# A reciprocal root changes places with a product in GpSimd's list

## The chip, the cores and the metric

The kernel runs on one core of one Trainium2 chip. The time is the device time of one execution in microseconds (us), as the median of several runs; lower is better. The engines are called PE (TensorE), DVE (VectorE), ACT (ScalarE), POOL (GpSimd) and SP (SyncE, which only starts transfers here). Each works through a list of its own in order and waits for the others through semaphores.

## The reference

Two layers over x of 16 sequences, 256 tokens, 128 features, in float32. Each layer is attention, then a feed-forward part; each part takes a layer norm scaled and shifted by a modulation, and adds its gated result to x. The first layer has softmax attention and 16 experts. The second, where the change lies, is

```
# holographic attention of layer 1, 16 heads of 64
k = exp(1j * (x @ Wk) * 10);  v = x @ Wv;  rotors = exp(1j * t * freqs)
out_pos   = real(cumsum(v * rotors) * conj(rotors)) / sqrt(t)
out_assoc = real(cumsum(v * conj(roll(k, 1))) * k) / sqrt(t)
x = x + ga * ((out_pos * g_pos + out_assoc * g_assoc) @ Wo)
# token mixing of layer 1
h = layernorm(x) * (1 + cb) + sb
x_prev = h shifted by one token
r = sigmoid((mu_r*h + (1-mu_r)*x_prev) @ W_r)
k = (mu_k*h + (1-mu_k)*x_prev) @ W_k
x = x + gb * (r * (square(relu(k)) @ W_v))
```

"The mixing" is this last part, and "its figures" are the mean and the reciprocal standard deviation of its layer norm.

## The kernel before

The 16 sequences are worked as 8 chunks of two (`NCH = 8`). Three stages follow each other: layer 0's attention, layer 0's experts, and layer 1 with both of its parts. The third runs from about 688 us to the end and is one loop over 58 steps `n`, each a chunk `c` and a group `j` of 128 of the 1024 head features. Chunks 0 to 5 have 7 groups here (one and a half of their groups were done ahead, in the experts' stage, and come back through `fetched`), chunks 6 and 7 have 8. The seventh group of chunks 0 to 5 is a half step (`is_half`): only its associative part is left.

In this stage all four engines' lists are in the order in which the code emits them (`manual_schedule(engines=IN_ORDER)`, line 1175). So the place of a call in the loop body is its place in the engine's list. For a step `n` the loop emits

- DVE: `summed` (L1238) twice, the running sums of the associative and of the positional binding; `phases(n + 2)` (L1213), the phase `off` of a later step; the product `m_pos` (L1450).
- POOL: the product `m` of step n - 1 (L1456), called `sum_assoc` in the profile; then `binders(n + 1)` (L1235), `bound_pos` and `bound_assoc` of the next step (a half step has only the latter). All are 128 x 1024.
- ACT: `cosines(n + 2)` (L1219 to L1221) makes the phasor from `off`, and `projected(n + 3)` (L1198, L1202) copies keys and values out of PSUM.
- PE: `out_project` for both products (L1252, into one accumulator per chunk) and the projections of step n + 3 (L1197, L1201). The next chunk's first `out_project` needs the accumulator, which `gated_out` on ACT (L1277, `oT`) reads out at j = 0.

Between these the mixing of earlier chunks is spread out: `place` maps a number of steps since a chunk's attention ended to that chunk, and each number has its piece of the mixing. Number 2 is `mix_means` (ACT, L204 and L205: sums of x and minus the mean, `less_f`). Number 3 is `mix_figures` (ACT, L213 to L221: sums of squares, then the variance plus epsilon, `off_f`). Number 4 is `mix_spread` (POOL, L228 the power of -1/2, called the root here, `rstd_f`; L229 its product with `less_f`). Number 5 is `mix_norm` (ACT, L236 through `normed`: `hn_f`). Then follow transposes (6), projections (7, 8, 9), gating (10, 11) and the output (12, 13).

`mix_spread` of number 4 is called near the end of the loop body, so its two small instructions come in POOL's list between the binders of one step and the product of the next. It is called for chunks 0 to 6 in this way. Chunk 7, the first to be mixed into x, has a call of its own at n = 5, and layer 0's stage calls the same function for the first layer norm of layer 1.

Of the kernel before, what the change touches and what calls it, by code (L numbers as in the profile page):

```python
# [55 lines left out]
def tile_adaln_two_layers(ctx: ExitStack, tc: tile.TileContext, a: dict, out: bass.AP):  # L56
# [167 lines left out]
    def mix_spread(c, pool):  # L224

        less, off = mix[c]
        rstd = pool.tile([P, 4], F32, tag="rstd_f1", name=f"rstd_f1_{c}")
        nc.gpsimd.tensor_tensor(rstd, off, neg_half4, ALU.pow)  # L228
        nc.gpsimd.tensor_tensor(less, less, rstd, ALU.mult)  # L229
        mix[c] = rstd, less  # L230
# [936 lines left out]
    with ExitStack() as scope:  # L1167
        hp = scope.enter_context(tc.tile_pool(name="holo", bufs=2))
# [54 lines left out]
        def is_half(n):  # L1223

            return steps[n][0] < AHEAD and steps[n][1] == NJ - 2
# [4 lines left out]
        def binders(n):  # L1230
            w = work[n]
            v2 = w["v"].unsqueeze(1).to_broadcast(both)
            for nm, bind in (("pos", rot(n)), ("assoc", phasor[n % 3][:, :, :, 0:T]))[is_half(n) :]:
                w[nm] = hp.tile(both, F32, tag=f"bound_{nm}", name=f"bound_{nm}_{n}")
                nc.gpsimd.tensor_tensor(w[nm], v2, bind, ALU.mult)  # L1235
# [101 lines left out]
        def mix_gated(c, k):  # L1337
            pv, r = mix[c], mix[c, "r"]
            nc.vector.tensor_tensor(r[:, k, :], pv[:, k, :], r[:, k, :], ALU.mult)
# [78 lines left out]
        for n in range(last + 2):  # L1418
# [3 lines left out]
            place = {n - begin[m + 1]: m for m in (c - 2, c - 1) if 0 <= m < NCH - 1 and n <= last}  # L1422
# [30 lines left out]
            if 1 <= n <= last + 1:  # L1453
                m = work.pop(n - 1)["m"]
                part = slice(1 if is_half(n - 1) else 0, 2)
                nc.gpsimd.tensor_tensor(m[:, part], m[:, part], phasor[(n - 1) % 3][:, part, :, 1:], ALU.mult)  # L1456
            if n + 1 <= last:
                binders(n + 1)
            if 1 <= n <= last + 1:
# [73 lines left out]
            for k in range(2):  # L1533
                if 10 + k in place:
                    mix_gated(place[10 + k], k)
            if 4 in place:
                mix_spread(place[4], hp)
            if 11 in place:
                py = with_tokens_first(place[11], mix.pop((place[11], "r")), "py2")
            for k in range(2):  # L1540
# [118 lines left out]
```

## Time and profile before

| | |
|---|---|
| median of three runs | 1080.41 us (1078.15, 1080.41, 1080.94) |
| the profiled execution | 1078.81 us |
| its span, first to last instruction | 1076.70 us |
| mean granted clock of PE | 0.996 |
| busy over the span | PE 1020.6 us (95%), DVE 912.8 (85%), POOL 796.8 (74%), ACT 704.4 (65%) |
| full products on POOL, spacing of their starts | about 2.13 us |
| root L228 on POOL, 15 in all | 0.997 to 1.274 us, median 1.024 |
| L229 on POOL, 15 in all | 0.20 us |
| distance of the roots at 851.10 and 894.92 | 43.82 us |

The span is what the trace covers; the execution's time has 2.11 us more around it. POOL's recorded durations overlap a little with the next start, so its speed is read from the distance of starts. A wait is the idle time of an engine ahead of an instruction, put down to the instruction elsewhere that ended last before it.

### The profile page before, as it was taken

How to read it: one execution, taken by the hardware profiler on the slowest of the kernel's cores; microseconds unless marked ns; L12 is line 12 of the kernel's file. 1: busy time of each engine (PE TensorE's matmuls, PEld its weight loads, DVE VectorE, ACT ScalarE, POOL GpSimd, SP SyncE). 2: the span in 40 equal slices, each digit the busy share in tenths (PEclk: the TensorE clock that was granted, in tenths of full speed). 3: DMA queues.
4: the chain of work that ended last, by engine and by line, in shares of the span. 5: the costliest groups of instructions: out<-in, count | busy, mean ns of one | idle time of the engine just before them, and what ended most of it. 6: DMA issues, size and time to landing. Idle time of an engine off the chain costs nothing.

```text
span 1076.7 us, 16224 instructions
## 1 busy us (share of the span) xinstructions
PE 1020.6 (95%) x5333; PEld 517.4 (48%) x5333; DVE 912.8 (85%) x1413; ACT 704.4 (65%) x1515; POOL 796.8 (74%) x754
## 2 busy tenths in 40 slices
PE   7999999999999999999999999898999999999987
PEld 5566666676654444444444434333344444444334
DVE  6679878998756798988878788999999999999995
ACT  3776677667656676687767755365676767767662
POOL 2245334533557678888878788899999999999992
PEclk9999999999999999999999999999999999999999
DMA  3102100000052222322322232100000000000000
GB/s 117 43 11 69 50 8 3 2 4 2 4 178 98 80 99 79 118 101 96 109 89 89 89 101 95 59 10 10 20 3 27 15 15 30 1 11 5 5 10 19
DMA packets 35538, 53.15 MB, mean 49 GB/s; under 512 B 8416, under 2 KB 23296, under 8 KB 35456
## 3 DMA queue, kind: packets, MB, share of 16 engines
q1 hardware_dynamic: 34912, 51.87, 14.9%
q8 instruction: 42, 0.69, 0.3%
q14 instruction: 40, 0.33, 0.1%
q10 hardware_dynamic: 544, 0.26, 0.1%
HBM read 46.34 MB, written 5.51 MB: 48 GB/s over the span
## 4 chain that ended last, share of the span: by engine, by line
PE 53%; POOL 20%; DVE 11%; ACT 8%; issue 6%; DMA 1%; SPq 0%; DVEq 0%; POOLq 0%; ACTq 0%
PE pg L808 6%; PE acc L833 6%; PE pup L810 6%; PE s L440 5%; PE st L474 5%; PE po L494 5%; PE pout L1252 4%; POOL bound_assoc L1235 4%; POOL sum_assoc L1456 4%; POOL bound_pos L1235 4%; POOL u L825 3%; DVE mem L1238 2%; DVE sum_assoc L1238 2%; PE pq L567 2%; PE pk L1197 1%
## 5 line engine op out<-in xcount | busy, mean ns | idle before, releaser
L482 ACT ACTIVATE exp<-st 128x512 f32<-128x512 f32 x256 | 132.2, 603 | 85.9 <-PE st L474 85.9
L452 DVE TENSOR_REDUCE maxima<-s 128x2 f32<-128x512 f32 x256 | 158.8, 683 | 25.9 <-PE s L440 25.6
L825 POOL TENSOR_TENSOR u<-u,wide 128x512 f32<-128x512 f32 x128 | 164.6, 1286 | 16.5 <-DVE u L824 7.4
L833 PE MATMUL acc<-u,w_dn 128*128 128x512 f32 x256 | 133.9, 605 | 6.1 <-POOL u L825 5.9
L1238 DVE TENSOR_TENSOR_SCAN sum_assoc<-keep,bound_assoc 128x1024 f32<-128x1024 bf16 (+1 forms) x58 | 125.8, 2168 | 12.8 <-POOL bound_assoc L1235 12.8
L808 PE MATMUL pg<-hT,w_gu 128*128 128x512 f32 x256 | 131.9, 597 | 0.8 <-DVE logits L674 0.4
L810 PE MATMUL pup<-hT,w_gu 128*128 128x512 f32 x256 | 130.7, 592 | 0.0
L814 ACT ACTIVATE u<-pup,b_gu 128x512 f32<-128x512 f32 x128 | 87.0, 680 | 63.6 <-PE pup L810 57.6
L1235 POOL TENSOR_TENSOR bound_assoc<-v,phasor 128x1024 f32<-128x1024 f32 x57 | 124.9, 2192 | 0.2 <-ACT phasor L1221 0.2
L818 POOL TENSOR_SCALAR u<-u 128x512 f32<-128x512 f32 x128 | 80.3, 628 | 59.6 <-ACT u L814 53.4
L812 DVE TENSOR_SCALAR g<-pg,b_gu 128x512 f32<-128x512 f32 x128 | 95.3, 745 | 32.7 <-PE pg L808 32.4
L1456 POOL TENSOR_TENSOR sum_assoc<-sum_assoc,phasor 128x1024 f32<-128x1024 f32 (+1 forms) x58 | 121.5, 2094 | 0.4 <-DVE sum_assoc L1238 0.3
L1238 DVE TENSOR_TENSOR_SCAN mem<-keep,bound_pos 128x1024 f32<-128x1024 bf16 x52 | 118.1, 2271 | 0.0
L1235 POOL TENSOR_TENSOR bound_pos<-v,rotor 128x1024 f32<-128x1024 f32 x51 | 111.7, 2189 | 0.0
L1252 PE MATMUL pout<-sum_assoc,w_assoc 128*128 128x512 f32 x228 | 108.1, 596 | 3.6 <-POOL sum_assoc L1456 3.6
L1252 PE MATMUL pout<-m_pos,w_pos 128*128 128x512 f32 x204 | 97.2, 599 | 15.0 <-ACT oT L1277 12.0
L817 ACT ACTIVATE pg<-g 128x512 f32<-128x512 f32 x128 | 76.3, 596 | 42.3 <-DVE g L812 41.9
L824 DVE SCALAR_TENSOR_TENSOR u<-u,pg 128x512 f32<-128x512 f32 x128 | 86.7, 677 | 11.9 <-POOL u L818 9.9
L1219 ACT ACTIVATE phasor<-off 128x512 f32<-128x512 f32 x56 | 35.1, 627 | 78.3 <-DVE off L1213 78.3
L474 PE MATMUL st<-qx,kx 32*128 32x256 f32 x1024 | 81.7, 387 | 1.2 <-DMA qx<-turned 1.1
L833 PEld LDWEIGHTS acc<-u,w_dn 128*128 128x128 f32 x256 | 46.7, 191 | 74.3 <-issue 42.9
L440 PE MATMUL s<-kx,qx 32*128 32x256 f32 x1024 | 78.1, 407 | 4.2 <-DVE kx L577 1.8
(301 smaller groups left out, 1910.0 us busy)
## 6 DMA issues: line engine op xcount, KB each, us to landing
wide<-scores SPq DMA_DIRECT2D x64, 512.0 KB
qx<-turned SPq DMA_DIRECT2D x256, 1.0 KB
there<-total SPq DMA_DIRECT2D x12, 256.0 KB
fetched<-there SPq DMA_DIRECT2D x12, 256.0 KB
w_gu<-in_gate_up_dram SPq DMA_DIRECT2D x8, 256.0 KB
out_dram<-x SPq DMA_DIRECT2D x16, 128.0 KB
x<-in_x_dram SPq DMA_DIRECT2D x14, 128.0 KB
w_dn<-in_down_dram SPq DMA_DIRECT2D x4, 256.0 KB
```

The source lines that it names most:

```text
L440: nc.tensor.matmul(s[g][:, i, :], qs[c][r][rows_, k, ts(i, P)], ks[c][rows_, r // NS, k, :], start=True, stop=True,)
L452: nc.vector.tensor_reduce(mx[:, :, g], s[g], AX.X, ALU.max, negate=True)
L474: nc.tensor.matmul(st[g][:, i, :], ks[c][rows_, r // NS, k, ts(i, P)], qs[c][r][rows_, k, :], start=True, stop=True,)
L482: nc.scalar.activation(e[:, g, :, :], st[g], AF.Exp, scale=QSCALE)
L808: nc.tensor.matmul(pg, w_gu[:, e, 0 : 2 * D : 2], h2, start=True, stop=True)
L810: nc.tensor.matmul(pu, w_gu[:, e, 1 : 2 * D : 2], h2, start=True, stop=True)
L825: nc.gpsimd.tensor_tensor(u, u, wide[n // SOME][:, n % SOME, :], ALU.mult)
L833: nc.tensor.matmul(accs[c], w_dn[:, e, :], work.pop(n), start=False, stop=(e == NE - 1))
L1235: nc.gpsimd.tensor_tensor(w[nm], v2, bind, ALU.mult)
L1238: nc.vector.tensor_tensor_scan(dst[:, half].rearrange("p s k t -> p (s k t)"), keep.rearrange("p (s k) t -> p s k t", k=2)[:, half].rearra ...
L1252: nc.tensor.matmul(pos[c], w[:, j, :], m[:, k, :, :].rearrange("p k t -> p (k t)"), start=(j == 0 and i == 0 and k == 0), stop=(c < NCH - ...
L1456: nc.gpsimd.tensor_tensor(m[:, part], m[:, part], phasor[(n - 1) % 3][:, part, :, 1:], ALU.mult)
```

## The change

The call of `mix_spread` for number 4 is taken out of the end of the loop body. The same call is made in the next step, where the chunk's number is 5, between the product L1456 of that step and `binders(n + 1)`.

```diff
                 nc.gpsimd.tensor_tensor(m[:, part], m[:, part], phasor[(n - 1) % 3][:, part, :, 1:], ALU.mult)
+            if 5 in place:
+                mix_spread(place[5], hp)
             if n + 1 <= last:
                 binders(n + 1)
...
-            if 4 in place:
-                mix_spread(place[4], hp)
             if 11 in place:
```

POOL's list around the root of one chunk, before and after:

```
before: bound_pos, bound_assoc | rstd_f, less_f | sum_assoc | bound_assoc of the half step
after:  bound_pos, bound_assoc | sum_assoc | rstd_f, less_f | bound_assoc of the half step
```

This holds at seven places (chunks 0 to 6). The calls for chunk 7 and in the experts' stage stay. The lists of the other engines have the same instructions in the same order; the first `hn_f` of each of the seven chunks carries a wait for POOL of its own, which before was covered by an earlier wait of ACT.

## The prediction

> **What bounds the kernel now.** I read the busy time of the engines by stage first. Every instruction that the change moves in a working place lies in the last stage, from 688 us on, so only that stage can gain.
>
> ```profile
> 688.00:1052.00 364.00, 337.05 (x831) 145.85 (x829) 350.81 (x283) 242.68 (x524) 356.61 (x183) 1.00 0.05 14
> ```
>
> The columns are the stretch, its length, and the busy us of PE, PE's weight loads, DVE, ACT and POOL. POOL is busy 356.61 of 364 us, DVE 350.81, PE 337.05. POOL comes nearest to setting the pace, so next I asked whom it waits for there (us in total, times, longest).
>
> ```profile
> POOL rstd_f L228 <- ACT off_f L221: 3.8, 5, 0.9
> POOL bound_assoc L1235 <- ACT phasor L1221: 0.2, 1, 0.2
> ```
>
> Nearly all of POOL's waiting is at the moved instruction: the root waits five times for ACT's off_f. The timeline shows one such place, on POOL, then on ACT (start, duration, instruction; in brackets the idle time before it).
>
> ```profile
> 889.86 2.22 POOL L1235 TENSOR_TENSOR bound_pos<-v,rotor 128x1024 f32<-128x1024 f32 x1
> 891.99 2.22 POOL L1235 TENSOR_TENSOR bound_assoc<-v,phasor 128x1024 f32<-128x1024 f32 x1
> 894.92 1.01 POOL L228 TENSOR_TENSOR rstd_f<-off_f,neg_half 128x4 f32<-128x4 f32 x1 [0.71 <-ACT off_f L221]
> 896.00 0.20 POOL L229 TENSOR_TENSOR less_f<-less_f,rstd_f 128x4 f32<-128x4 f32 x1
> 896.36 2.17 POOL L1456 TENSOR_TENSOR sum_assoc<-sum_assoc,phasor 128x1024 f32<-128x1024 f32 x1 [0.16 <-issue]
> 898.50 2.18 POOL L1235 TENSOR_TENSOR bound_assoc<-v,phasor 128x1024 f32<-128x1024 f32 x1
> ```
>
> ```profile
> 890.95 0.72 ACT L1221 ACTIVATE phasor<-off,half_pi 128x512 f32<-128x512 f32 x1
> 894.64 0.20 ACT L221 ACTIVATE off_f<-off_f 128x4 f32<-128x4 f32 x1
> 903.34 1.66 ACT L236 ACTIVATE hn_f<-x,less_f,rstd_f 128x128 f32<-128x128 f32 x4
> ```
>
> POOL stands 0.71 us until off_f ends at 894.84. The product behind it (L1456) had nothing to wait for: DVE's sums for it ended about 891.2. The five waits, read off the same timeline, begin before the roots at 807.29 (0.74), 851.10 (0.72), 894.92 (0.71), 938.92 (0.72) and 983.23 (0.93): 3.82 us. The roots at 763.51 and 1035.67 wait for nothing. The root at 724.78 is not moved.
>
> Last I asked who else is nearly late. Per chunk DVE waits once, for POOL, and PE once, for ACT:
>
> ```profile
> 907.12 2.29 DVE L1238 TENSOR_TENSOR_SCAN sum_assoc<-keep,bound_assoc 128x1024 f32<-128x1024 bf16 x1 [1.55 <-POOL bound_assoc L1235]
> 916.08 1.98 PE L1252 MATMUL pout<-m_pos,w_pos 128*128 128x512 f32 x4 [1.86 <-ACT oT L1277]
> 960.39 1.98 PE L1252 MATMUL pout<-m_pos,w_pos 128*128 128x512 f32 x4 [1.42 <-ACT oT L1277]
> 980.13 2.18 POOL L1235 TENSOR_TENSOR bound_assoc<-v,phasor 128x1024 f32<-128x1024 f32 x1 [0.24 <-ACT phasor L1221]
> 983.23 1.01 POOL L228 TENSOR_TENSOR rstd_f<-off_f,neg_half 128x4 f32<-128x4 f32 x1 [0.93 <-ACT off_f L221]
> ```
>
> This closes a loop per chunk: POOL's binder releases DVE, DVE's off releases ACT's cosines, values and oT, oT releases PE, PE's next projections pace ACT, ACT's off_f releases POOL's root.
>
> **The change, part by part.** It adds and removes no work. Seven pairs (L228 and L229, about 1.24 us) trade places on POOL with the product of one step earlier; no DMA moves and SP's list is the same. The other engines keep their order.
>
> *The wait taken away.* After the change POOL goes from the binder (end 894.2) straight into the product, 2.13 us by the spacing of the starts. Only then does it ask for off_f, which is by then 1.4 us old (2.13 less 0.71). So the five waits go: 3.82 us at most.
>
> *Who reads the root later.* less_f would end 0.71 us earlier than the product ended before (898.53), near 897.8. Its reader, ACT's hn_f, starts at 903.34. This edit costs nothing: 5.5 us of cover, filled by ACT's cosines and evictions. Without the cover ACT would stop at L236, with the next cosines behind it and POOL's binder behind those.
>
> *What is late next.* The loop has a part that doesn't pass through POOL: PE's list of a chunk, then pv to ACT's v and oT and back to PE. In the chunk at 960.39 PE itself was what ACT waited for, and its gap was 1.42 us, so I take 1.42 as the shortest hand-over. The other chunks' gaps are 1.86, 1.85 and 1.86 (at 828.26, 872.07 and 916.08), so PE can come forward by only 0.44, 0.43 and 0.44 there, and not at all at 960.39. Its whole lead is thus 0.44, 0.87, 1.31 and 1.31 us.
>
> POOL meets this two instructions ahead of the root, at the binder that needs ACT's cosine L1221, which PE's list paces. At 891.99 the cosine had ended at 891.67, so POOL was 0.32 behind it; in the row at 980.13, where POOL did wait, start less cosine's end (979.98) is 0.15. The difference, 0.17 us, is the slack; it is the same in the chunks at 848.18 and 935.99. So POOL's lead there can't exceed PE's by more than 0.17. Now chunk by chunk, POOL's lead:
>
> - root at 807.29: +0.74; next binder caps it at 0.44 + 0.17 = 0.61.
> - root at 851.10: 0.61 + 0.72 = 1.33; capped at 0.87 + 0.17 = 1.04.
> - root at 894.92: 1.04 + 0.71 = 1.75; capped at 1.31 + 0.17 = 1.48.
> - root at 938.92: 1.48 + 0.72 = 2.20. Here the next binder (942.28) is near its cosine too: ACT has hT's modulation in front of it and ends at 941.68, 0.60 ahead, so a slack of 0.45: capped at 1.31 + 0.45 = 1.76. The binder at 980.13 has no slack: capped at 1.31.
> - root at 983.23: 1.31 + 0.93 = 2.24.
>
> From there POOL has no gap until 1051.9, and DVE, which waits for POOL at 990.96 (1.35) and again up to 1049.84 (0.59), follows. So 2.24 of the 3.82 us are kept, 1.58 go into waits for the cosine. The 0.16 us marked "issue" behind one root I leave alone, since the list may be interrupted elsewhere.
>
> *Bounds.* If PE can't come forward at all, POOL keeps only the last 0.93. If PE's hand-over holds nothing, all 3.82 go, and the 0.16 and 0.24 at most with them: 4.22. I take 2.24, which the 1.42 row is nearest to.
>
> *A rule that would speak against it.* The product now starts 2.2 us earlier beside DVE and meets m_pos (893.85) instead of the scan alone. The Trainium skill (SBUF — State Buffer, "Who interferes with whom") states that a DVE instruction with two SBUF inputs and a GpSimd instruction that reads SBUF block each other for a whole instruction. Here m_pos takes its sum from PSUM, so by the rule too there is no block, and the sum stays; by the rule for two SBUF inputs it would be the last rival below. The trace's own row: of 58 products the longest lasts 2.230 us against a median of 2.181, whatever DVE ran.
>
> **The rivals.**
>
> *All of the gain.* ACT and PE follow POOL fully, because the 1.42 at 960.39 belongs to a chunk with other work in it (hT's modulation, two more norms). For: PE is busy 337 of 364 us, less than DVE. Against: PE's list between the gaps shows no idle time. It gives 3.82 to 4.22, so 1076.4.
>
> *The wait only moves.* The binders' cosine wait takes back all but the last root's part: 0 to 0.93 us, 1079.9. For: 0.17 us of slack. Against: PE's gaps do exceed 1.42.
>
> *Slower.* The product in its new slot is blocked by DVE's m_pos, or blocks it, one m_pos each (1.21 us) at seven roots: 8.5 less 2.2 gives +6.2, so 1086.6. It decides as soon as a product that starts within m_pos is stretched by over 0.3 us. Against: the product at 868.52 starts inside the m_pos of 868.10 and lasts 2.20.
>
> **How the numbers follow.** The profiled execution took 1078.81 us, 2.11 around its span of 1076.70; the sum gives 1076.57 for it. It lay 1.60 below the median of the three runs, 1080.41, which gives 1078.17 for a median. All four executions average 1079.58, less 2.24 is 1077.3. I forecast 1077.8, between the two.
>
> 0.3% is 3.24 us, about what a measurement of this kernel tells from no change. Forecast (gain 0.93 to 3.2): 0.50. All of the gain: 0.31. Only moved: 0.14. Slower: 0.05. The runs differ by 2.8 us among themselves, so about three in ten of the forecast's case would show as over 0.3%: 0.15, and nine in ten of the full gain: 0.28, in all 0.43 faster. Slower gets its 0.05 and 0.01 of the third case. The rest, 0.51, is within 0.3%. Range: from 1080.41 less 4.22 and 0.8 of scatter, 1075.4, to 1080.41 less 0.93 and 0.7 of scatter, 1080.2.
>
> **What would show it.** Right: no wait of rstd_f for off_f in the last stage; new waits of bound_assoc for phasor L1221 of some 0.1 to 0.5 us, five or six; PE's gap before pout near 1.4 in each chunk; a distance of roots of 43.4 us instead of 43.8. Wrong: no such waits and a gap before pout near 1.1 (all of the gain), products over 2.5 us (the lock), hn_f waiting for less_f, or root and off_f still waiting.

## The result and the profile after

| | before | changed |
|---|---|---|
| median, 22 runs each | 1080.2 us (1077.61 to 1084.27) | 1077.01 us (1075.34 to 1080.66) |
| ratio to before, 95% interval | | 0.9972 [0.9961, 0.9983] |
| span of the profiled execution | 1076.7 us | 1073.6 us |
| POOL's part of the last stage | 361.63 us | 359.07 us |

The changed kernel is faster by 0.28%, some 3.0 us (1.8 to 4.2 by the interval). The last row runs from the start of the stage's first `bound_pos` (690.58 and 690.01) to the start of the last full product (1052.21 and 1049.08). It leaves out the stages in front, which the change doesn't touch; 0.57 us of the 3.1 us between the two spans lie there. So 2.56 us were gained where the change is. Of the runs of the kernel before that stand beside the experiments below, one took 3632 us; it is left out of their ratios.

POOL's waits in the last stage, changed kernel (us in total, times, longest):

```profile
POOL bound_assoc L1235 <- ACT phasor L1221: 1.7, 4, 0.8
```

The line for `rstd_f` and `off_f` (3.8 us, five times) is gone. In its place the binder waits for the cosine: 1.7 us instead of 0.2. POOL's idle time accounts for the gain: 3.81 us of waits for `off_f` and a hole of 0.16 us (marked "issue") go, and the waits for the cosine grow by 1.42, from 0.24 to 1.66. That makes 2.55 us of the 2.56. The timeline of the chunk shown before, POOL and then ACT:

```profile
890.32 2.18 POOL L1235 TENSOR_TENSOR bound_assoc<-v,phasor 128x1024 f32<-128x1024 f32 x1 [0.25 <-ACT phasor L1221]
892.46 2.18 POOL L1456 TENSOR_TENSOR sum_assoc<-sum_assoc,phasor 128x1024 f32<-128x1024 f32 x1
894.59 1.01 POOL L228 TENSOR_TENSOR rstd_f<-off_f,neg_half 128x4 f32<-128x4 f32 x1
895.68 0.20 POOL L229 TENSOR_TENSOR less_f<-less_f,rstd_f 128x4 f32<-128x4 f32 x1
```

```profile
889.45 0.72 ACT L1221 ACTIVATE phasor<-off,half_pi 128x512 f32<-128x512 f32 x1
893.14 0.21 ACT L221 ACTIVATE off_f<-off_f 128x4 f32<-128x4 f32 x1
901.42 1.65 ACT L236 ACTIVATE hn_f<-x,less_f,rstd_f 128x128 f32<-128x128 f32 x4
```

The root now starts 1.24 us after `off_f` has ended (893.35) and has no idle time ahead of it. `less_f` ends at 895.88, 5.5 us before `hn_f` reads it. POOL stands 0.25 us at the binder, 0.14 us behind the cosine's end (890.175). PE at one gap before, and at three after:

```profile
872.07 1.98 PE L1252 MATMUL pout<-m_pos,w_pos 128*128 128x512 f32 x4 [1.85 <-ACT oT L1277]
```

```profile
870.57 1.98 PE L1252 MATMUL pout<-m_pos,w_pos 128*128 128x512 f32 x4 [1.42 <-ACT oT L1277]
913.91 1.98 PE L1252 MATMUL pout<-m_pos,w_pos 128*128 128x512 f32 x4 [1.42 <-ACT oT L1277]
958.23 1.98 PE L1252 MATMUL pout<-m_pos,w_pos 128*128 128x512 f32 x4 [1.42 <-ACT oT L1277]
```

The gaps of 1.85 and 1.86 have shrunk to 1.42, the one that had been 1.42 is still 1.42, and the first two rows after are 43.34 us apart instead of 44.0.

### The profile page after: what moved, and what is told of

Its sections match the earlier page's. It is cut to its first block, busy times and chain, and to the rows that moved or that the text cites. A ratio compares the mean times of both kernels' runs of the same rounds, so it can differ in the third digit from the quotient of the medians.

```text
span 1073.6 us, 16224 instructions
## 1 busy us (share of the span) xinstructions
PE 1020.8 (95%) x5333; PEld 518.4 (48%) x5333; DVE 913.2 (85%) x1413; ACT 705.0 (66%) x1515; POOL 796.7 (74%) x754
## 4 chain that ended last, share of the span: by engine, by line
PE 64%; POOL 15%; DVE 10%; issue 5%; ACT 5%; DMA 1%; SPq 0%; DVEq 0%; POOLq 0%; ACTq 0%
PE pout L1252 9%; PE pg L808 7%; PE acc L833 7%; PE pup L810 7%; PE s L440 5%; PE st L474 5%; PE po L494 5%; POOL u L825 3%; POOL bound_assoc L1235 3%; POOL bound_pos L1235 3%; POOL sum_assoc L1456 2%; PE pk L1197 2%; PE pv L1201 2%; DVE sum_assoc L1238 2%; DVE mem L1238 2%
## 5 line engine op out<-in xcount | busy, mean ns | idle before, releaser
L1456 POOL TENSOR_TENSOR sum_assoc<-sum_assoc,phasor 128x1024 f32<-128x1024 f32 (+1 forms) x58 | 120.9, 2085 | 0.3 <-DVE sum_assoc L1238 0.3
```

## The experiments

The theory is that of the prediction: a loop from PE through ACT back to PE, with a hand-over of 1.42 us per chunk, paces the cosines and takes back part of what POOL gains. All stages below are measured as in the table above. The experiments' medians were taken in two groups (the first four and the last three), each beside runs of the kernel before of its own, so only the ratios compare across rows. A stage is read from one profiled run of each kernel.

| kernel | stage, us | ratio to before |
|---|---|---|
| before | 361.63 | 1 |
| changed | 359.07 | 0.9972 [0.9961, 0.9983] |
| e1_out_early | 358.20 (0.88 of it at its entry) | 0.9945 [0.9933, 0.9957] |
| e2_out_early_root_old | 357.55 | 0.9951 [0.9939, 0.9963] |
| e3_root_behind_binders | 360.89 | 0.9984 [0.9973, 0.9995] |
| e4_no_root | 357.79 (entry differs, see there) | 0.9942 [0.9929, 0.9955] |
| e5_all_but_last | 359.97 | 0.9977 [0.9964, 0.9989] |
| e6_only_last | 360.68 | 0.9991 [0.9976, 1.0006] |
| e7_no_root_out_early | 351.56 | 0.9894 [0.9873, 0.9914] |

In the seven kernels that leave nothing out (before, changed, e1, e2, e3, e5 and e6) the stage less POOL's idle stretches of over 0.1 us is 357.0 to 357.2 us. So to within some 0.1 us the stages of these seven differ by POOL's waits alone.

**e1_out_early: take the hand-over away.** `gated_out` moves in ACT's list from behind the cosines of its step to a place ahead of them.

```diff
+            if j == 0 and c:
+                o = gated_out(c - 1)
             if n + 2 <= last:
                 if n == 0:
                     phases(n + 2)
                 cosines(n + 2)
...
-            if j == 0 and c:
-                o = gated_out(c - 1)
```

> The changed kernel, and gated_out (ACT, oT) moved in ACT's list ahead of the cosines of its step, into ACT's idle time of about 2.5 us. Measure: POOL's stage, from the first bound_pos of the stage to the start of the last sum_assoc product (before 361.63 us, changed kernel 359.07). Theory (a loop PE, ACT, PE with a hand-over of 1.42 us paces the cosines and so POOL): PE's gaps of 1.42 before pout go, the four waits of bound_assoc for the cosine (1.66 us) go, stage 357.4, about 1.7 us less time than the changed kernel. Rival (the waits come from ACT's own load or from DVE): the waits stay within 0.3 us of what they were, stage 359.1.

No wait for the cosine is left, and no gap before pout that waits for oT. In the changed kernel ACT stood idle just ahead of these cosines:

```profile
866.27 0.63 ACT L1219 ACTIVATE phasor<-off 128x512 f32<-128x512 f32 x1 [1.58 <-DVE off L1213]
```

In e1_out_early, ACT (first row) and PE at the same chunk, and POOL's wait at the stage's entry:

```profile
865.17 0.84 ACT L1277 ACTIVATE oT<-pout,gaT 128x256 f32<-128x256 f32 x2 [1.07 <-PE pout L1252]
868.40 1.88 PE L1252 MATMUL pout<-m_pos,w_pos 128*128 128x512 f32 x4
693.95 2.17 POOL L1456 TENSOR_TENSOR sum_assoc<-sum_assoc,phasor 128x1024 f32<-128x1024 f32 x1 [0.88 <-DVE sum_assoc L1238]
```

`oT` now runs where ACT had been waiting for DVE, and ends (866.01) 2.4 us before PE starts the pout that needs the accumulator (868.40). The stage is 358.20; the 0.88 us at its entry, where POOL came earlier than DVE, belong to no chunk and without them it is 357.3. The rival, that ACT's own load or DVE causes the cosine's lateness, falls: ACT and DVE have the same work, and only the place of oT on ACT differs. The interval of e1_out_early lies wholly below the changed kernel's. Of the kernels that leave nothing out, this one and the next are the fastest; their intervals overlap.

**e2_out_early_root_old: the other cut of the same loop.** The edit of e1_out_early, made in the kernel before.

> The kernel before, with the root in its old place, and oT ahead of the cosines as in e1_out_early. Theory (the root's wait and the hand-over lie in one loop, which either edit cuts): off_f comes early enough, rstd_f waits for nothing in the stage, stage 357.4, the same as e1_out_early within 0.3 us. Rival (off_f is late by the order of ACT's own list, whatever PE does): rstd_f still waits 3 us or more in all, stage 361 or more.

The root waits for nothing in its old place and the stage is 357.55, 0.2 us from e1's 357.3; a hole of 0.15 us ahead of one product accounts for most of that. With PE's hand-over gone, `off_f` comes in time and the root's place no longer matters. So the root's wait was the loop's slowness seen on POOL.

**e3_root_behind_binders: one place too late.**

```diff
-            if 5 in place:
-                mix_spread(place[5], hp)
             if n + 1 <= last:
                 binders(n + 1)
+            if 5 in place:
+                mix_spread(place[5], hp)
```

> The changed kernel with the root one place later still, behind the next binders. Theory (the root in front of the half step's binder fills time that the binder would spend waiting for its cosine): the half step's bound_assoc waits for the cosine, 0.4 to 0.9 us in each of three chunks and 1.2 to 1.8 in the chunk of 940 us; stage 360.0 to 360.8, slower than the changed kernel by 1 to 1.7 us. Rival (any place behind the product is as good): 359.1, the same.

Two of the four waits of the half step's binder on POOL:

```profile
898.31 2.18 POOL L1235 TENSOR_TENSOR bound_assoc<-v,phasor 128x1024 f32<-128x1024 f32 x1 [0.84 <-ACT phasor L1221]
942.91 2.18 POOL L1235 TENSOR_TENSOR bound_assoc<-v,phasor 128x1024 f32<-128x1024 f32 x1 [1.49 <-ACT phasor L1221]
```

They are 0.57, 0.59, 0.84 and 1.49 us. At 898.31 the binder starts 0.43 us behind its cosine's end, at the other three 0.14, so some 0.29 us of the 0.84 are not the cosine's. The stage is 1.82 us longer than the changed kernel's, 0.09 above the expected range. Behind the product is not enough: in front of the binders the root fills time in which the binder's cosine is still being made.

**e4_no_root: take 8.7 us off POOL.** This kernel leaves the root and its product out of the norm of seven chunks. It doesn't compute the reference and only serves to load POOL less.

```diff
             if 5 in place:
-                mix_spread(place[5], hp)
+                mix[place[5]] = mix[place[5]][::-1]
```

> The changed kernel without the two small POOL instructions of chunks 0 to 6 (the mixing's layer norm is scaled by the variance and shifted by minus the mean instead of by the root and its product). Takes 7 x 1.24 = 8.7 us of work off POOL. Theory (PE's loop paces the chunks between 827 and 958 us): the distance of PE's pout behind the gap stays 43.34 us per chunk there, the time goes into longer waits of bound_assoc for the cosine, and only 3 to 5 us are gained on the changed kernel: stage 354 to 356. Rival (POOL's list alone paces the stage): 8.7 us gained, stage 350.4.

POOL's waits, and PE at the two ends of the four chunks that PE paces in the changed kernel:

```profile
POOL bound_assoc L1235 <- ACT phasor L1221: 8.6, 10, 1.7
```

```profile
789.20 1.98 PE L1252 MATMUL pout<-m_pos,w_pos 128*128 128x512 f32 x4 [1.42 <-ACT oT L1277]
963.55 1.98 PE L1252 MATMUL pout<-m_pos,w_pos 128*128 128x512 f32 x4 [1.42 <-ACT oT L1277]
```

These are 174.35 us apart; in the changed kernel the same two (783.89 and 958.23) are 174.34 apart. Four roots fewer on POOL change nothing there: the binder's waits grow from 1.7 to 8.6 us. Behind 963.55 the last product starts 88.53 us later, against 90.85: 2.32 us gained, about the two roots (2.5) that lie there. The stage of 357.79 misses the expected 354 to 356. About 1.0 us of that is the entry (from the first `bound_pos` to the pout at 789.20 it takes 94.91 us, against 93.88), the rest an estimate of the gain that was too high. What made the entry longer is open; the profiled run was the slowest of this kernel's six (1078.68 us, median 1074.57).

**e5_all_but_last and e6_only_last: the gain by places.** The first leaves only chunk 5's root in its old place, the second moves only that one.

```diff
             if 5 in place:
-                mix_spread(place[5], hp)
+            if 5 in place and place[5] != 5:
+                mix_spread(place[5], hp)
...
+            if 4 in place and place[4] == 5:
+                mix_spread(place[4], hp)
```

> The root is in its new place for all chunks but number 5, whose root (at 983 us) stays in its old place in front of the product. Stage measured as before (before 361.63 us, changed kernel 359.07). Theory (the first four roots gain what PE's loop allows, 1.6 us, and the last one adds its whole wait of 0.93 because PE's loop has no say behind it): rstd_f waits once, about 0.9, bound_assoc before it about 0.76 for the cosine; stage 360.0. Rival (the loop of the chunk of 960 us takes back all of the first four): stage 361.6, the time of the kernel before.

> Only the root of chunk 5 stands in its new place, the others in their old one. Theory: the four earlier waits of 0.71 to 0.74 stay, the one of 0.93 goes and nothing takes it back; stage 360.7, 0.9 less than before. Rival (only the last root matters): 359.1, as the changed kernel.

POOL in e5_all_but_last, in the chunk of 960 us:

```profile
978.24 2.18 POOL L1235 TENSOR_TENSOR bound_assoc<-v,phasor 128x1024 f32<-128x1024 f32 x1 [0.78 <-ACT phasor L1221]
981.34 1.01 POOL L228 TENSOR_TENSOR rstd_f<-off_f,neg_half 128x4 f32<-128x4 f32 x1 [0.92 <-ACT off_f L221]
```

The four earlier roots gain 361.63 - 359.97 = 1.66 us of the 2.89 that they had waited; the last one alone gains 361.63 - 360.68 = 0.95, its whole wait. Together 2.61, measured together 2.56. The medians can't tell so little (e6's interval includes 1); the stage lengths can.

**e7_no_root_out_early: both.** The edits of e1_out_early and e4_no_root together.

> e4_no_root (without the two small POOL instructions of chunks 0 to 6, the mixing's layer norm scaled by the variance) with oT ahead of the cosines as in e1_out_early. Theory (with the hand-over gone POOL sets the pace, so work taken off POOL counts): 4 to 7 us less stage than e1_out_early (358.2, of which 0.9 is a wait at the stage's entry), until DVE's waits of 0.6 per chunk for POOL are used up; stage 351 to 354. Rival (as in e4_no_root POOL's work hardly counts): 1 to 2.5 us less than e1_out_early, stage 355.5 to 357.

The stage is 351.56 us: 6.6 below e1_out_early, 5.8 without its entry. The same 8.7 us off POOL that took 1.3 us off the changed kernel's stage (2.3 without the longer entry of e4_no_root) take 5.8 off this one. POOL's waits hold the rest:

```profile
POOL bound_assoc L1235 <- ACT phasor L1221: 2.3, 3, 1.1
POOL sum_assoc L1456 <- DVE sum_assoc L1238: 0.9, 1, 0.9
```

The second is the last product's; it was 0.27 us in e1_out_early. So 2.3 and 0.6 us went into waits, and 5.8 and 2.9 make the 8.7. The rival, that POOL's work hardly counts, falls.

## Why the prediction came out right

*The wait taken away.* Right: all five waits of the root went, and every product in the new slot ran at the usual 2.18 us (longest of all 2.200). The "slower" rival, a block between the product and DVE's m_pos, had its chance: all seven products ahead of the moved roots start while an m_pos runs. They last 2.16 to 2.18 us and these m_pos 1.22, so neither is held.

*Who reads the root later.* Right: 5.5 us of cover were predicted, 5.5 measured.

*What is late next.* Right in mechanism and place. The hand-over of 1.42 us, taken from one row, holds in each of the four chunks. Lead over the kernel before, both counted from the stage's first `bound_pos` (from rows rounded to 0.01 us):

| place (time before) | predicted | measured |
|---|---|---|
| PE at 828.26, 872.07, 916.08, 960.39 | 0.44, 0.87, 1.31, 1.31 | 0.46, 0.93, 1.60, 1.59 |
| POOL's binder at 848.18, 891.99, 935.99 | 0.61, 1.04, 1.48 | 0.64, 1.10, 1.76 |
| POOL's binder at 942.28, 980.13 | 1.76, 1.31 | 2.11, 1.59 |
| the last product | 2.24 | 2.56 |

The mis-sized term is the chunk before 916.08: PE gained 0.67 us there, not 0.44. The prediction read PE's list between the gaps as free of idle time. In this chunk of the kernel before it was not, as a weight load of PE (PEld) shows:

```profile
912.23 0.30 PEld L1197 LDWEIGHTS pk<-hT,w_k 128*128 128x128 f32 x2 [0.78 <-DVE off L1213]
```

PE's pk products behind it start at 912.24 and its pv products at 913.20, which is 0.98 and 0.96 us behind the rows ahead of them; in the changed kernel both distances are 0.86. These 0.22 us are nearly the whole difference of 0.23. They fit the hole of 0.16 us marked "issue" on POOL, which the prediction left alone: DVE waited 1.55 us for POOL in this chunk (907.12), against 1.37 and 1.35 in its neighbours (863.12 and 950.92). The hole stands in all three kernels that have this root in its old place (before, e2_out_early_root_old and e6_only_last, 0.155 to 0.157 us). In e3, e4 and e7 the half step's binder of the same chunk starts 0.43 us behind its cosine's end instead of the usual 0.14. The changed kernel, e1 and e5 show neither. What makes the hole is open.

The waits for the cosine came where the caps put them. The caps give 0.13, 0.29, 0.27, 0.44 and, with the 0.24 that was there before, 0.69 us. The profile lists 0.25, 0.26, 0.39 and 0.76; the first one shows only as a spacing of 2.21 us at 846.97, against 2.13. So the sign "five or six waits of 0.1 to 0.5" was met in place, with one wait longer and one hardly to be seen.

*The rivals.* "All of the gain" is refuted by the changed kernel's gaps and shown to need the hand-over's removal: e1 and e2 reach it. "The wait only moves" is a part of what happened: of the 3.8 us of waits, 1.4 moved to the cosine.

*The time.* The forecast was 1077.8, the median 1077.01. Of the 0.8 between them 0.3 are the chunk above. The rest is where the forecast put itself between runs that differ by 2.8 us. The medians alone don't bear the mechanism out: their gain of 1.8 to 4.2 us holds the forecast's 2.24 and the 3.82 of "all of the gain" as well. The rows of the stage tell the two apart. That 0.28% fell on the likelier side of the 0.3% is luck, since the interval reaches from 0.17% to 0.39%.

## What to carry to other kernels

An in-order engine that waits at a small instruction can gain about that wait by a reordering, and keeps what the next slowest loop allows. Walk the list on to the next cross-engine wait and measure its slack before booking the gain. Here the gap that was shortest, in the one chunk where its engine had waited for nothing else, was that loop's floor: 1.42 us before, and 1.41 to 1.42 in every chunk that PE paced after. Once such a loop is found, cut it where that is cheapest: reading out the accumulator in ACT's idle time, ahead of the cosines, took 4.1 us off the stage where moving the root took 2.6, and with it the root could have stayed.

## What the runs showed of the hardware

Part of the scatter between runs goes with PE's granted clock. Of e5_all_but_last's twelve runs, the six with 0.997 took 1076.26 to 1076.87 us, the three with 0.986 or 0.987 took 1078.34 to 1078.89. It isn't all: the two with 0.995 took 1078.05 and 1078.19, and of e1_out_early's five, the one with 0.991 took 1073.57 us and the one with 0.994 took 1076.58. The stage's first `bound_pos` starts between 688.76 and 694.29 us in these nine profiles, although no kernel was changed in front of it. What sets this was not tried. A stage's length between two marks leaves this out: the two parts of the gain add up to the whole within 0.05 us, where e6's median can't be told from no change. Each is from one profile, though, and the stage's entry alone differed by 0.9 and 1.0 us in two of them (e1_out_early, e4_no_root).

The hand-over from PE over ACT's value copy and oT back to PE took 1.41 to 1.42 us wherever it was shortest, in all six kernels that have oT in its old place (before, changed, e3 to e6). POOL's power of -1/2 on 128 x 4 took 1.0 us, half as long as a product of 128 x 1024 at 2.13.
